# A third buffer for scan states, narrower room for background work on ScalarE, and wider rows in DRAM, in a fused four-layer kernel

## Chip, cores and metric

The kernel runs on one core of one Trainium2 chip. The metric is the device time of one execution in microseconds (us). All data are 32-bit floats. An image is one of the 16 batch entries.

## The reference

Four layers follow each other, each of the form x + layer(group norm of x), on x of 16 x 192 x 32 x 32. Only layers 1 to 3 bear on this change. Cut to what matters:

```python
x = x + _L0_conv_ref(_gn(x), ...)      # gated recurrent block, 3x3 convolution, batch norm
x = x + _L1_conv_ref(_gn(x), ...)      # channel attention: 1x1 and depthwise 3x3 convolutions
x = x + _L2_conv_ref(_gn(x), ...)      # selective scan, below
x = x + _L3_conv_ref(_gn(x), ..., 4)   # softmax over rolled copies of x, 1x1 convolution, gelu

# inside layer 2: xs is xx in K = 4 directions, 384 channels, N = 16 states, L = 1024 steps
x_dbl = einsum('bkdl,kcd->bkcl', xs, x_proj_w)
dts, Bs_, Cs_ = split(x_dbl, [R, R + N], axis=2)
delta = softplus(einsum('bkrl,kdr->bkdl', dts, dt_w) + dt_b)
def step(h, xs_t):
    d_t, u_t, B_t, C_t = xs_t
    dA = exp(d_t[..., None] * A)
    h = h * dA + (d_t * u_t)[..., None] * B_t[:, :, None, :]
    y = einsum('bkdn,bkn->bkd', h, C_t)
    return (h, y)
```

## The kernel before

Layer 0 is run first for all images. The rest is the class `LayersB`. `prepare` (L1132) makes, for one image, layer 1 and the start of layer 2, up to the scan's input `xx` (after a Gelu) and the gate `z`. The scan follows. `complete` (L1358) makes the end of layer 2 and layer 3.

The scan of one image is 192 slots (`UNITS`, L748): 4 directions x 24 groups of 16 channels x 2 blocks of 8 states. A slot is one scan instruction on 128 x 1024. Its partitions are 16 channels x 8 states and its free axis is the 1024 steps. Two slots, an even "first" one and an odd "second" one, make a pair and share a group of channels. Per pair the engines do this, each engine in the order of the program:

- SyncE loads `dl` and `du` (`load_group`, L1793): 16 rows of 4 KB in DRAM, each read 8 times, 512 KB into SBUF each. The two loads for a later pair are issued in the second slot (`fetch`, L1802).
- ScalarE makes `dA` = exp(`dl` x A) for each slot, two slots ahead (`decay`, L1835), and copies `du` into one of the two PSUM buffers `xt` (`inputs_up`, L1831). This copy is issued in the second slot and can begin when the scan of the first slot has read that buffer.
- VectorE multiplies `xt` by the state inputs `bb` twice (L1842), then runs the two scans into `h` (L1851). There are two buffers `h`.
- GpSimd multiplies `h` by the state outputs `cb` into `hc` (L1863, three buffers), one slot behind the scan.
- TensorE sums `hc` over the states into `acc` (L1893), two slots behind. ScalarE copies `acc` out (L1903) every fourth slot.

The scan of image b runs beside the background: `prepare` of image b + 1 and `complete` of image b - 1, two Python generators ("streams") that are cut into pieces by `yield`. A piece names the engine that it uses next. The order of all instructions is written out when the program is built (`scans`, L1618), and the engines follow it: a piece that is emitted in a slot stands behind that slot's own work on its engine. There is no choice at run time.

The planner keeps a clock in us for each engine. `SLOT` (L754) is the planned length of the first and the second slot (4.83 and 2.31), `RATES` in `Metered` (L764) the planned cost of an instruction. `fits` (L1687) lets a piece into a slot if its engine's clock is under the slot's end plus `OVER` (one number for first slots, one for second), if its input is due, with `LEAST` us to spare, before that end, and for TensorE and VectorE if the slot's budget `ALLOW` is not yet spent. An early loop (L1633) lets ScalarE pieces in ahead of the slot's own work by the same test. Pieces marked "late" (those with Tanh or Gelu) go into second slots only.

Two due times are not left to `fits`. In slot 161 of an image (`FETCH`, L749), the loop at L1664 emits all pieces of `prepare` of the next image that are still outstanding, up to its Gelu of `xx`, because `fetch_xx` (L1354) then loads `xx` for the next scan. In slot 144 the loop at L1668 emits all pieces of `complete` up to its second read of `yd`, because the scan overwrites `yd` from there on. After the last slot of the last image the loop at L1680 emits what is left of `complete` of the image before. One background stream has one PSUM bank (`mm`, L836), so a matmul group of a stream waits until ScalarE or VectorE has read the one before.

Steps of the next direction (`front`, L1728: projection, softplus into `dlh`, product into `duh`, stores to `dld` and `dud`) are placed at fixed slots. They use `e`, `dlh` and `duh`, 2 KB per partition each.

Of the kernel before, what the change touches and what calls it, by code (L numbers as in the profile page):

```python
# [11 lines left out]
F32 = mybir.dt.float32  # L12
# [7 lines left out]
C, H, W = 192, 32, 32  # L20
L = H * W
HL = L // 2
P6 = 96
# [4 lines left out]
K, N, R = 4, 16, 12  # L28
# [13 lines left out]
class Ctx:  # L42
# [22 lines left out]
    def ln_exp(self):  # L65
# [4 lines left out]
        if self.ordered:  # L70
            self.spent["ACT"] += TABLE
        i = self.nc.scalar.preload_act_table_set("natural_log_exp_and_others")
# [672 lines left out]
BLOCKS = N // NBL  # L745
# [8 lines left out]
SLOT = (4.83, 2.31)  # L754
OWN = {"POOL": 2.36, "SUMS": 0.6, "START": 0.9, "INPUTS": 1.0, "DECAY": 1.15, "COLLECT": 0.57}
ENGINES = ("PE", "ACT", "POOL", "DVE")
ALLOW = {"PE": 2.45, "DVE": 0.3}
OVER = {"PE": (0.8, 1.2), "ACT": (0.0, 1.5), "POOL": (0.5, 1.5)}
LEAST = {"PE": 1.0, "ACT": 0.6, "POOL": 0.8}
TABLE = 1.28  # L760
MARGIN = 0.6


class Metered:  # L764


    RATES = {"ACT": (0.07, 0.00105), "POOL": (0.1, 0.0022), "DVE": (0.08, 0.00105), "PE": (0.06, 0.0017)}
    LEAST = {"ACT": 0.2, "POOL": 0.2, "DVE": 0.12, "PE": 0.4}

# [3 lines left out]
    def __getattr__(self, op):  # L773
        f = getattr(self.engine, op)

        def issue(out, *args, **kw):
            base, each = self.RATES[self.name]
            self.spent[self.name] += max(self.LEAST[self.name], base + each * math.prod(out.shape[1:]))
            if op == "activation" and args[1] in (AF.Tanh, AF.Gelu):
                self.spent["ACT"] += TABLE * self.cx.has_ln  # L780
                self.cx.has_ln = False
# [43 lines left out]
class LayersB:  # L825
# [44 lines left out]
    def run(self):  # L870
        tc, NB = self.tc, self.NB
        self.bank, self.turn = None, 0
        with ExitStack() as ctx:
# [4 lines left out]
            self.xp = ctx.enter_context(tc.tile_pool(name="b_x", bufs=1, space=PSUM))  # L878
            self.spent, self.have = dict.fromkeys(ENGINES, 0.0), dict.fromkeys(ALLOW, 0.0)
            self.clock = dict.fromkeys(ENGINES, 0.0)  # L880
# [26 lines left out]
    def setup(self):  # L907

        tc, nc, cx, wp, I, NB = self.tc, self.nc, self.cx, self.wp, self.I, self.NB
        dp = self.dp  # L910
        self.dqd = dp.tile([6, 128, 9, 128], F32, name="dqd")
        self.dvd = dp.tile([2, 2, P6, 9, P6], F32, name="dvd")
        self.vd = dp.tile([P6, 2, L], F32, name="vd")
        self.x0d = dp.tile([P6, 2, L], F32, name="x0d")
        self.x2d = dp.tile([P6, 2, L], F32, name="x2d")
        self.xdr = dp.tile([K, 2 * N, L], F32, name="xdr")
        self.dld = dp.tile([K, 3, 128, L], F32, name="dld")
        self.dud = dp.tile([K, 3, 128, L], F32, name="dud")
        self.xxd = dp.tile([3, 128, L], F32, name="xxd")
        self.yd = dp.tile([3, 128, L], F32, name="yd")  # L920
        self.zd = dp.tile([NB, 3, 128, L], F32, name="zd")
        self.x1d = dp.tile([NB, P6, 2, L], F32, name="x1d")


        bn_g, bn_b = self.vec("bn_g", P6), self.vec("bn_b", P6)
        self.bsc = wp.tile([P6, 2], F32, name="bsc")
        self.bsh = wp.tile([P6, 2], F32, name="bsh")
        with tc.tile_pool(name="b_pre0", bufs=1) as pre:
            st = pre.tile([P6, 2, NB, 12], F32, name="st")
            for a in range(2):  # L930
                nc.scalar.dma_start(
                    st[:, a], self.sdram[:, a * P6 : (a + 1) * P6, :].rearrange("b p s -> p b s")
                )
            mv = pre.tile([P6, 2, 2], F32, name="mv")
            for a in range(2):
                nc.vector.bn_aggr(mv[:, a, :], st[:, a].rearrange("p b s -> p (b s)"))
            sd = pre.tile([P6, 2], F32, name="sd")
            nc.scalar.activation(sd, mv[:, :, 1], AF.Sqrt, bias=cx.eps5[0:P6])
            nc.vector.reciprocal(sd, sd)
            nc.vector.tensor_mul(self.bsc, sd, bn_g)  # L940
            nc.vector.tensor_mul(sd, mv[:, :, 0], self.bsc)
            nc.vector.tensor_sub(self.bsh, bn_b, sd)


        self.offb = wp.tile([P6, P6], F32, name="offb")
        nc.sync.dma_start(self.offb, I["c_off48"])
        self.temp = wp.tile([P6, 2], F32, name="temp")
        for a in range(2):
            for j in range(2):
                nc.sync.dma_start(  # L950
                    self.temp[48 * j : 48 * j + 48, a : a + 1],
                    I["temperature"][2 * a + j : 2 * a + j + 1].unsqueeze(0).to_broadcast([48, 1]),
                )

        self.dw2b = self.vec("dw_b", 128)
        self.pads = [wp.tile([128, H + 2, W + 2], F32, name="pad%d" % i) for i in range(2)]
        for t in self.pads:
            nc.gpsimd.memset(t, 0.0)

        self.xx = wp.tile([128, 3, L], F32, name="xx")  # L960
    def setup_scans(self):

        nc, cx, wp, I = self.nc, self.cx, self.wp, self.I
# [50 lines left out]

        ring = lambda name, n, shape: [wp.tile(shape, F32, name=name + str(i)) for i in range(n)]
        self.y = wp.tile([128, 3, L], F32, name="y")
        self.dA, self.h, self.hc = ring("dA", 3, [128, L]), ring("h", 2, [128, L]), ring("hc", 3, [128, L])
        self.dl, self.du = ring("dl", 2, [128, L]), ring("du", 2, [128, L])
        self.bb, self.cb = ring("bb", BLOCKS, [128, L]), ring("cb", 3, [128, L])
        self.e, self.dlh, self.duh = (wp.tile([128, HL], F32, name=n) for n in ("e", "dlh", "duh"))  # L1020
        self.xd = wp.tile([64 + XR, L], F32, name="xd")
        self.dtw = wp.tile([64 + R, INNER], F32, name="dtw")
        self.xt = [self.xp.tile([128, L], F32, name="xt%d" % i) for i in range(2)]
# [108 lines left out]
    def prepare(self, b):  # L1132

        nc, cx, sm, I = self.be, self.cx, self.sm, self.I
# [42 lines left out]
        for m in range(3):  # L1177
# [5 lines left out]
            elif m == 1:  # L1183
                w1 = self.weight(self.w1d, [P6, 2, C])
            else:
                wpf = self.weight(I["w_projfT"].rearrange("(a p) o -> p a o", p=P6), [P6, 2, C])
# [13 lines left out]

        id6 = cx.ident[0:P6, 0:P6]
        at = sm.tile([P6, 2, P6], F32, tag="at", name="at", bufs=1)
        kk = sm.tile([P6, 2, C], F32, tag="m1", name="kk", bufs=1)[:, :, 0:P6]
        rq = sm.tile([P6, 2], F32, tag="rq", name="rq")
        vs = [self.p4([P6, 2, HL], "vh") for _ in range(2)]
        for hf in range(2):
# [19 lines left out]
        for a in range(2):  # L1226
# [5 lines left out]
                nc, pk[:, ch(a)], [(qT[:, t, k0 : k0 + P6], qT[:, t, k0 : k0 + P6]) for t in range(NCH)]  # L1232
            )
        yield "DVE", 0
        nc.vector.tensor_mul(
            kk, pk.rearrange("p (a c) -> p a c", a=2), id6.unsqueeze(1).to_broadcast([P6, 2, P6])
        )
# [34 lines left out]
        yield "ACT", 0  # L1272
        for a in range(2):
            nc.scalar.mul(at[:, a, :], at[:, a, :], den[:, a : a + 1])
        m1 = sm.tile([P6, 2, C], F32, tag="m1", name="m1", bufs=1)
        m2 = sm.tile([P6, 2, C], F32, tag="m2", name="m2", bufs=1)
        for m_, w_ in ((m1, w1), (m2, wpf)):
            yield "PE", 0
            p = self.mm()[0:P6, 0 : 2 * C]
            for a in range(2):  # L1280
                nc.tensor.matmul(p[:, a * C : (a + 1) * C], lhsT=at[:, a, :], rhs=w_[:, a, :], start=True, stop=True)
            yield "ACT", 0
            nc.scalar.copy(m_, p.rearrange("p (a c) -> p a c", a=2))
        ds = [self.taps(P6, self.dvd[1, 0], I["dw_kv"][ch(0)], b == 0)]
        for hf in range(2):
            for a in range(2):
# [331 lines left out]
    def scans(self, b, more, carry):  # L1618
# [9 lines left out]
        for t in range(UNITS):  # L1628
# [30 lines left out]
            for e in ENGINES:  # L1659
                clock[e] += self.spent[e] - was[e]  # L1660
            for e in ALLOW:
                have[e] = min(have[e], 0.0) + ALLOW[e] - self.spent[e] + was[e]
            if more and t == FETCH:
# [23 lines left out]
    def fits(self, s, end):  # L1687

        if not s.open(self.slots) or s.engine == "SP":
            return s.engine == "SP" and s.open(self.slots)  # L1690
        at = self.clock[s.engine]
        if s.engine != "DVE":
            end += OVER[s.engine][self.slots % BLOCKS]
        wait = s.inputs()
        if wait > at and (s.engine == "DVE" or wait + LEAST[s.engine] > end):
            return False
        return at < end + 0.1 and self.have.get(s.engine, 1.0) > 0.0

# [145 lines left out]
    def scan(self, u):  # L1844
        nc = self.nc
        n, blk = divmod(u, BLOCKS)
        k = n // GROUPS
        views = [self.h[u % 2], self.dA[u % 3], self.xt[(n + 1 + blk) % 2]]
        if k >= 2:
            views = [v[:, ::-1] for v in views]  # L1850
        nc.vector.tensor_tensor_scan(*views, 0.0, op0=ALU.mult, op1=ALU.add)  # L1851

    def outputs(self, u, carried=False):

        n, blk = divmod(u, BLOCKS)

        k = n // GROUPS - K * (carried and u == UNITS - 1)
        views = [self.hc[u % 3], self.h[u % 2], self.c_of(k, blk)]
        if n // GROUPS % 2:
            views = [views[0].rearrange("p (h w) -> p w h", w=W)] + [  # L1860
                v.rearrange("p (w h) -> p w h", h=H) for v in views[1:]
            ]
        self.nc.gpsimd.tensor_mul(*views)  # L1863
# [139 lines left out]
```

## Time and profile before

| What | us |
|---|---|
| Median of 3 runs (15584.52 to 15626.19) | 15609.16 |
| Profiled execution, its own time | 15591.93 |
| Profiled execution, its span | 15590.1 |
| First scan of layers 1 to 3 starts at | 3545.2 |
| Last scan of layers 1 to 3 ends at | 15451.2 |
| From the last scan's end to the end of the span | 138.9 |
| Granted TensorE clock, mean over the span | 0.838 |

The 3072 scans take 11906 us, so a pair of slots takes 7.75 us on average; the median pair takes 7.42 us and the fastest tenth 6.83 us. Before them lie layer 0, the un-interleaved `prepare` of image 0 and the first steps of its scan; after them `complete` of the last image. In the profile, most background instructions have line L782, that of the helper that records their cost, and have to be told apart by their tiles. A matmul of 32-bit floats has two records, so 18 records on `pad` are one half of a 3x3 depthwise convolution (9 matmuls).

### The profile page before, as it was taken

To read this page: it belongs to the slowest core of one execution; us is meant where nothing else is said; L and a number is where in the kernel's file an instruction comes from. 1 tells how busy PE (TensorE), PEld (TensorE's weight loads), DVE (VectorE), ACT (ScalarE), POOL (GpSimd) and SP (SyncE) were. 2 spreads that over 40 slices of the span, in tenths; PEclk is the share of its full clock that TensorE was granted. 3 is DMA by queue.
4 is the path that set the end of the run, shared out by engine and by line. 5 is a ranking of instruction groups with operands and counts; after the bars stand their busy time and mean duration, and the time that the engine had idled before them with its cause. 6 is when DMAs were issued, how large, how long until landed. Compare 5 with 4: busy or idle time off the path is not lost. (4 is left out here: it accounts for less than half of the span.)

```text
span 15590.1 us, 196674 instructions
## 1 busy us (share of the span) xinstructions
PE 12621.5 (81%) x72384; PEld 5045.6 (32%) x72384; DVE 12310.8 (79%) x10295; ACT 9263.9 (59%) x12084; POOL 9861.8 (63%) x5787
## 2 busy tenths in 40 slices
PE   9999999987787777877787777877787777878755
PEld 5555555542222222222222222222222222222212
DVE  4444444448988999999989898898989898988997
ACT  3333333326666666666666666666666666666665
POOL 1000000006787878787878787878878787878785
PEclk9999999997787888878788888887888887878766
DMA  1000000017777787878787878787777787777775
GB/s 29 12 15 14 15 14 15 15 40 189 201 195 200 188 207 188 210 182 214 182 211 183 213 184 211 183 210 189 202 194 198 194 202 195 199 195 193 201 182 129
DMA packets 852126, 2412.70 MB, mean 155 GB/s; under 512 B 114352, under 2 KB 234240, under 8 KB 843520
## 3 DMA queue, kind: packets, MB, share of 16 engines
q1 hardware_dynamic: 838496, 2397.64, 60.2%
q8 instruction: 580, 9.50, 0.3%
q10 hardware_dynamic: 12704, 2.72, 0.1%
q14 instruction: 346, 2.83, 0.1%
HBM read 2018.92 MB, written 364.30 MB: 153 GB/s over the span
## 5 line engine op out<-in xcount | busy, mean ns | idle before, releaser
L1863 POOL TENSOR_TENSOR hc<-h,cb 128x1024 f32<-128x1024 f32 x3072 | 7247.3, 2371 | 2046.2 <-DVE h L1851 1557.8
L1851 DVE TENSOR_TENSOR_SCAN h<-dA,xt 128x1024 f32<-128x1024 f32 x3072 | 6912.8, 2273 | 297.0 <-POOL hc L1863 289.1
L1842 DVE TENSOR_TENSOR xt<-xt,bb 128x1024 f32<-128x1024 f32 x3072 | 3633.4, 1227 | 852.7 <-ACT xt L1831 718.9
L1835 ACT ACTIVATE dA<-dl,A 128x1024 f32<-128x1024 f32 x3072 | 3506.7, 1146 | 801.2 <-DMA dl<-dld 672.8
L1893 PE MATMUL acc<-hc,sel 128*32 128x256 f32 x24576 | 2406.8, 473 | 1707.6 <-POOL hc L1863 1705.0
L782 PE MATMUL mm<-pad,dg 128*128 128x512 f32 (+1 forms) x5580 | 2899.3, 655 | 13.3 <-ACT pad L782 9.9
L1831 ACT COPY xt<-du 128x1024 f32<-128x1024 f32 x1536 | 1557.6, 1014 | 1361.7 <-DVE h L1851 1183.5
L1893 PEld LDWEIGHTS acc<-hc,sel 128*32 128x32 f32 x24576 | 562.2, 120 | 4055.4 <-POOL hc L1863 2897.2
L782 PEld LDWEIGHTS mm<-pad,dg 128*128 128x128 f32 (+1 forms) x5580 | 995.5, 192 | 1479.2 <-issue 1363.3
L596 POOL TENSOR_TENSOR vw<-va,gtok 128x396 f32<-128x396 f32 x112 | 95.2, 850 | 1712.0 <-ACT va L588 1712.0
L782 PE MATMUL mm<-x,wgt 96*128 96x512 f32 (+1 forms) x1664 | 1064.5, 775 | 140.1 <-ACT o L782 50.0
L1884 PE MATMUL acc<-y,ident 128*128 128x512 f32 x576 | 445.7, 866 | 445.5 <-ACT y L1903 444.5
L782 POOL TENSOR_TENSOR t<-x 96x768 f32<-96x768 f32 (+4 forms) x510 | 647.5, 1290 | 204.6 <-PE mm L782 204.2
L691 POOL TENSOR_TENSOR x_in<-x_in,sz 128x384 f32<-128x384 f32 x128 | 116.8, 913 | 750.5 <-DVE x_in L687 676.7
L782 PE MATMUL mm<-d,xT 128*96 128x256 f32 x2048 | 569.1, 416 | 5.6 <-ACT o L782 5.3
L782 PEld LDWEIGHTS mm<-x,wgt 96*128 96x128 f32 (+1 forms) x1664 | 342.1, 226 | 669.9 <-issue 364.5
L782 POOL TENSOR_TENSOR duh<-dlh,xx 128x512 f32<-128x512 f32 x384 | 537.5, 1400 | 30.1
L782 POOL TENSOR_TENSOR dlh<-dlh,e 128x512 f32<-128x512 f32 x384 | 488.4, 1272 | 103.1 <-ACT e L782 101.2
L782 PE MATMUL mm<-xd,dtw 12*128 12x512 f32 x768 | 534.5, 782 | 10.0 <-ACT z L782 10.0
L622 DVE TENSOR_TENSOR D<-D,s 128x256 f32<-128x256 f32 x768 | 270.8, 415 | 322.6 <-ACT D L619 322.6
L389 PE MATMUL pc<-ypad,w_c 128*64 128x512 f32 (+1 forms) x1152 | 442.9, 633 | 80.4 <-PEq L735 41.3
L619 ACT ACTIVATE D<-s 128x256 f32<-128x256 f32 x768 | 232.7, 390 | 426.3 <-PE s L613 426.3
(331 smaller groups left out, 15374.9 us busy)
## 6 DMA issues: line engine op xcount, KB each, us to landing
dl<-dld SPq DMA_DIRECT2D x1536, 512.0 KB
du<-dud SPq DMA_DIRECT2D x1536, 512.0 KB
dld<-dlh SPq DMA_DIRECT2D x384, 256.0 KB
dud<-duh SPq DMA_DIRECT2D x384, 256.0 KB
bb<-xdr SPq DMA_DIRECT2D x128, 512.0 KB
cb<-xdr SPq DMA_DIRECT2D x128, 512.0 KB
dg<-dqd SPq DMA_DIRECT2D x270, 192.0 KB
zd<-z SPq DMA_DIRECT2D x48, 512.0 KB
```

The lines of the kernel that those rows point to most:

```text
L389: nc.tensor.matmul(p[r, :], lhsT=w_, rhs=v, start=(n == 0), stop=(n == 14))
L619: nc.scalar.activation(d, S[j][:, two], AF.Exp)
L622: nc.vector.tensor_mul(d, d, S[j][:, 2 * CH :])
L691: nc.gpsimd.tensor_mul(hT[:, :, cs], hT[:, :, cs], sz[:, :, cs])
L782: return f(out, *args, **kw)
L1831: self.nc.scalar.copy(self.xt[n], self.du[n])
L1835: self.nc.scalar.activation(self.dA[u % 3], self.dl[n % 2], AF.Exp, scale=self.A[:, blk, n : n + 1])
L1842: self.nc.vector.tensor_mul(self.xt[(n + 1 + blk) % 2], self.xt[n % 2], self.bb[blk])
L1851: nc.vector.tensor_tensor_scan(*views, 0.0, op0=ALU.mult, op1=ALU.add)
L1863: self.nc.gpsimd.tensor_mul(*views)
L1884: nc.tensor.matmul(acc, lhsT=self.cx.ident, rhs=self.y[:, g, half(pair)], start=True, stop=False)
L1893: nc.tensor.matmul(self.acc[rows4(q), q4(s)], lhsT=self.sel[:, m, :], rhs=self.hc[u % 3][:, q4(q)], start=False, stop=(s + m + blk == 3),)
```

## The change

There are five edits.

1. `h` gets a third buffer, and `scan` and `outputs` take `h[u % 3]`.
2. Room in SBUF is made for it: `e` becomes the same buffer as `duh`; the small tile `kk` moves to the slot "pa", and `m1` and `m2` move to the ring "w" of two weight buffers, which holds `w1` and `wpf` before them and `wx` and `wz` after them.
3. The planner's numbers for ScalarE in first slots change: a piece must find ScalarE's clock 0.6 us before the slot's end where the end itself was enough, and an input that comes later than the clock must be due 1.6 us before that, where it was 0.6.
4. TensorE's budget per slot goes from 2.45 to 3.0 us.
5. Rows of `xdr`, `dld` and `dud` in DRAM lie 36 KB apart (`PITCH` = 9 rows of 4 KB), where they were 4 KB apart. The bytes that are moved stay the same.

```diff
-ALLOW = {"PE": 2.45, "DVE": 0.3}
-OVER = {"PE": (0.8, 1.2), "ACT": (0.0, 1.5), "POOL": (0.5, 1.5)}
-LEAST = {"PE": 1.0, "ACT": 0.6, "POOL": 0.8}
+ALLOW = {"PE": 3.0, "DVE": 0.3}
+OVER = {"PE": (0.8, 1.2), "ACT": (-0.6, 1.5), "POOL": (0.5, 1.5)}
+
+LEAST = {"PE": (1.0, 1.0), "ACT": (1.6, 0.6), "POOL": (0.8, 0.8)}
 TABLE = 1.28
+PITCH = 9
...
-        self.xdr = dp.tile([K, 2 * N, L], F32, name="xdr")
-        self.dld = dp.tile([K, 3, 128, L], F32, name="dld")
-        self.dud = dp.tile([K, 3, 128, L], F32, name="dud")
+
+        self.xdr = dp.tile([K, 2 * N, PITCH, L], F32, name="xdr")[:, :, 0, :]
+        self.dld = dp.tile([K, 3, 128, PITCH, L], F32, name="dld")[:, :, :, 0, :]
+        self.dud = dp.tile([K, 3, 128, PITCH, L], F32, name="dud")[:, :, :, 0, :]
...
-        self.dA, self.h, self.hc = ring("dA", 3, [128, L]), ring("h", 2, [128, L]), ring("hc", 3, [128, L])
+        self.dA, self.h, self.hc = ring("dA", 3, [128, L]), ring("h", 3, [128, L]), ring("hc", 3, [128, L])
...
-        self.e, self.dlh, self.duh = (wp.tile([128, HL], F32, name=n) for n in ("e", "dlh", "duh"))
+        self.dlh, self.duh = (wp.tile([128, HL], F32, name=n) for n in ("dlh", "duh"))
+        self.e = self.duh
...
-        kk = sm.tile([P6, 2, C], F32, tag="m1", name="kk", bufs=1)[:, :, 0:P6]
...
+        kk = self.slot("pa", [P6, 2, P6], "kk")
...
-        m1 = sm.tile([P6, 2, C], F32, tag="m1", name="m1", bufs=1)
-        m2 = sm.tile([P6, 2, C], F32, tag="m2", name="m2", bufs=1)
-        for m_, w_ in ((m1, w1), (m2, wpf)):
+
+        ms = []
+        for w_ in (w1, wpf):
...
+            m_ = self.slot("w", [P6, 2, C], "m", 2)
+            ms.append(m_)
             nc.scalar.copy(m_, p.rearrange("p (a c) -> p a c", a=2))
+        m1, m2 = ms
...
-        if wait > at and (s.engine == "DVE" or wait + LEAST[s.engine] > end):
+        if wait > at and (s.engine == "DVE" or wait + LEAST[s.engine][self.slots % BLOCKS] > end):
             return False
...
-        views = [self.h[u % 2], self.dA[u % 3], self.xt[(n + 1 + blk) % 2]]
+        views = [self.h[u % 3], self.dA[u % 3], self.xt[(n + 1 + blk) % 2]]
...
-        views = [self.hc[u % 3], self.h[u % 2], self.c_of(k, blk)]
+        views = [self.hc[u % 3], self.h[u % 3], self.c_of(k, blk)]
```

## The prediction

> **What bounds the kernel now.** I read the busy times of the stretches first. The scan loop runs from 3545.2 to 15451.2 us; the row above it is the un-interleaved `prepare` of image 0. Columns: length, then busy us of TensorE, its weight loads, VectorE, ScalarE, GpSimd (instructions in brackets), granted TensorE clock, DMA share, GB/s.
>
> ```profile
> 3354.00:3518.00 164.00, 147.34 (x393) 67.24 (x394) 85.68 (x157) 41.77 (x77) 0.21 (x1) 0.92 0.20 59
> 3545.20:15451.20 11906.00, 9189.66 (x42510) 3203.20 (x42510) 10736.22 (x7133) 7882.74 (x9506) 9524.81 (x5243) 0.80 0.77 196
> ```
>
> VectorE is busy for 10736 of 11906 us. It is the bound, and what can be won is its idle time. The waits of VectorE in that window say who ends it (total, times, longest):
>
> ```profile
> DVE xt L1842 <- ACT xt L1831: 689.2, 355, 8.1
> DVE h L1851 <- POOL hc L1863: 289.1, 229, 3.3
> DVE yh L782 <- PE mm L782: 36.8, 16, 3.3
> DVE xt L1842 <- DMA bb<-xdr: 17.7, 32, 3.2
> ```
>
> With the small rows this is 1039 us. The 289 us are scans that wait for a free `h`. The 689 us are the copy of `du` being late on ScalarE. The timeline shows how that comes about (start, length, instruction, idle time before it and who ended it):
>
> ```profile
> 4640.88 5.43 PE L782 MATMUL mm<-pad,dg 96*96 96x512 f32 x6
> ...
> 4646.35 0.58 ACT L782 COPY vf<-mm 96x512 f32<-96x512 f32 x1 [8.73 <-PE mm L782]
> ...
> 4646.83 1.02 ACT L1831 COPY xt<-du 128x1024 f32<-128x1024 f32 x1
> ...
> 4647.88 2.36 DVE L1842 TENSOR_TENSOR xt<-xt,bb 128x1024 f32<-128x1024 f32 x2 [7.04 <-ACT xt L1831]
> ```
>
> A background copy stands ahead of the scan's copy on ScalarE and waits 8.73 us for a convolution on TensorE; VectorE then idles 7.04 us. I went through the 355 waits this way: some 430 us have ScalarE waiting for TensorE in a background piece, 55 us have it waiting for `dl`.
>
> [...] a record on `pad` takes 592 ns in the median and up to 1223. [...] Edit 5 goes from 4 to 36 KB, [...] and no run here shows it. [...]
>
> **Part by part. Third `h`.** The scan may now be one slot further ahead of GpSimd, at least 2.3 us (one scan, 2273 ns). Of 229 waits three quarters are under 1.95 us, and the longest is 3.3. About 60 of the 289 us stay. It goes on to wait for GpSimd only when GpSimd is two slots late.
>
> **ScalarE in first slots.** The copy gets at least 1.0 to 1.6 us more slack before a background piece. Taking 1.6 us off each of the 355 waits leaves 278 of 689 us. In the order of the changed kernel's instructions, some 460 background ScalarE pieces are let into first slots by `fits`, where 706 were; 278 x 460 / 706 = 180. With 60 for the other rows (yh, bb, small ones), 60 + 180 + 60 = 300 of 1039 us stay. Bounds: 150 (all waits for ScalarE go) to 600 (TensorE, up to 8 us late, is too late for 1.6 us to matter).
>
> **What that order also shows.** A stricter door slows both streams; TensorE's larger budget (3.0) does not help a stream that waits for ScalarE. Counted between the sums of two neighbouring slots, the kernel before never has more than 9 background matmuls. The changed kernel keeps to 11 in images 0 to 4, then falls behind, and the due times empty the streams at one place:
>
> - slot 161 (`prepare` is due): 20, 40, 68, 94, 122, 124, 112, 124, 124, 124 matmuls in images 5 to 14
> - slot 144 (`complete` is due): 37, 53, 83, 83, 83, 13 in images 10 to 15
> - after the last slot: 156
>
> In the kernel before, no piece is forced by a due time. A forced block is one dependent chain: one bank for each stream, so TensorE waits for ScalarE's copy, ScalarE for TensorE. TensorE's next sums, ScalarE's next `dA` and copy, and VectorE's next scan (behind the block's own VectorE pieces) are queued behind it. VectorE can run two more slots under a block at 161 and one under a block at 144, because their `dA` and `xt` were emitted before it; then it stands still.
>
> Price of a matmul of 512 columns, from `prepare` of image 0 (36 records are 18 matmuls, 15.62 / 18 = 0.87 us):
>
> ```profile
> 3446.97 15.62 PE L782 MATMUL mm<-pad,dg 96*96 96x512 f32 x36
> ...
> 3482.80 7.89 PE L782 MATMUL mm<-pad,dg 128*128 128x512 f32 x18
> ```
>
> TensorE: by columns the blocks at 161 make 17 + 35 + 57 + 80 + 103 + 104 + 96 + 3 x 104 = 804 us, those at 144 make 25 + 32 + 3 x 49 + 11 = 215. That is 1019 us at full clock and 1108 at the 0.92 of the stretch alone. ScalarE: 197 and 81 forced pieces, at 0.58 us for a copy of 512, 1.05 to 1.23 for 1024 wide, 1.28 for a table load: 183 + 78. VectorE: 48. GpSimd: 133, mostly beside TensorE because those pieces are pipelined; a third counts, 45. Handovers: some 680 changes of engine at 0.12 us, the mean of 0.04 (TensorE to ScalarE) and 0.2 (back) as the last `complete` shows them: 82. Sum 1108 + 261 + 48 + 45 + 82 = 1544. Off it come ten times 7 us and seven times 2.3 us of scans that run under a block (86), and VectorE's 48, which the loop's busy time already holds: 1410 us.
>
> A check on one block: 3438.5 to 3518 us is about the block of 124 matmuls, made alone, 79.5 us, with half of five convolutions on VectorE beside TensorE. Put back on TensorE they add 5 x (7.89 + 0.58) = 42, together 122 us with three banks in turn; my sum has about 150 for one bank. So the low bound is 0.82 of the sum: 1544 x 0.82 - 134 = 1130. The high bound takes TensorE at the loop's clock of 0.80: 1410 + 166 = 1576.
>
> **The end.** 156 matmuls by columns 66 us, ScalarE 27, a part of GpSimd's 50 and handovers: 110 us (90 to 130), after the last scan and so all on the path.
>
> **`fetch_xx` after a block.** `xxd` is written only at the block's end, so SyncE waits for that store before it can load `xx`, and the next `dl` and `du` stand behind it on SyncE's queue. 1.5 MB out and in at the loop's 196 GB/s is 8 + 8 us, of which about 10 us of scans hide most: 6 us a block, 60 us (0 to 120).
>
> **The rest.** `e` in `duh`: the next `e` is written three slots after `duh`'s store was issued, some 11 us: nothing; were the store later, ScalarE would wait. `kk`, `m1`, `m2` in other slots: `wx` and `wz` load after `m1` and `m2` were read, once an image, and SyncE waits a few us with `dl` behind it: within the bounds above. Row pitch: the waits of VectorE that a faster `dl` or `bb` would end are 55 + 18 us, so at best -70; at worst the loads slow until they bind, which I bound by +100. I take nothing.
>
> **Sum.** 15592 (the profiled execution) - 1039 + 300 + 1410 + 110 + 60 = 16433 us. The median of the runs lies 17 us above the profiled one: 16450. Low: 15592 - 1039 + 150 + 1130 + 90 + 17 = 15940. High: 15592 - 1039 + 600 + 1576 + 130 + 120 + 17 = 16996.
>
> **Rivals.**
> - *Faster: the blocks are mostly hidden.* In images 5 and later the planner's clocks stay ahead after a block, so dozens of slots carry no background and TensorE is free there. If the engines could begin a block well before VectorE reaches its slot, 60 in 100 of it would be under scans: 15592 - 1039 + 300 + 0.4 x 1580 + 17 = 15502. It decides once blocks, end and fetch cost under 739 - 17 us together. Against it: the block stands behind sums of slot 159, which need its scan, so it cannot begin early. 0.06.
> - *Half clock in the blocks.* [...] TensorE's 1019 us double (2340 instead of 1410) and its 66 at the end too: 15592 - 1039 + 300 + 2340 + 176 + 60 + 17 = 17446. Against it: the stretch alone held 0.92. 0.08.
> - *The door does not help.* ScalarE's waits stay because TensorE is late by much more than 1.6 us: 750 instead of 300 stay, 16900. For it: waits up to 8.1 us. Against it: later images have less background outside the blocks. 0.14.
>
> **How the numbers follow.** My forecast, with sizes between its bounds, has 0.72. The range 15950 to 16980 holds it but for its tails, and the third rival; outside lie the first two rivals and some tails, 2 in 10. Within 0.3% of 15609 (about what a measurement of this kernel can tell from no change) needs gain and blocks to cancel: 0.03, out of the low tail. Faster 0.06, slower 0.91.
>
> **What would show it.** Right: in images 0 to 4 the scan takes some 30 us less than the 748 us that an image took before (by the starts of every 192nd scan); in images 9 to 14 it takes 100 to 200 us more; VectorE has a few idle stretches of 60 to 150 us near slots 144 and 161; the time from the last scan to the end grows from 139 to about 250; the row of `h` waiting for `hc` falls under 100 us. Wrong: if those stretches are under 40 us each, or if the first five images don't get shorter.

## The result, and the profile after

| Kernel | Median us | Runs | Ratio to before, 95% interval |
|---|---|---|---|
| before | 15599.7 (15584.52 to 15626.19) | 4 | |
| changed | 17019.26 (17004.21 to 17028.31) | 4 | 1.0897 [1.0884, 1.091] |

The change makes the kernel 1420 us slower. The forecast was 841 us slower than the 15609 it started from; the measured time lies 39 us above its range.

First the busy times of two stretches of the changed kernel, the scan loop and what follows it. The columns are those of the prediction.

```profile
3545.70:16760.20 13214.50, 9293.80 (x42216) 3256.72 (x42220) 10699.57 (x7127) 7892.17 (x9468) 9468.89 (x5178) 0.75 0.68 177
16760.20:17011.70 251.50, 168.79 (x708) 85.17 (x700) 47.43 (x83) 82.38 (x121) 77.79 (x108) 0.72 0.09 27
```

The loop is 1308.5 us longer and the end 112.6 us longer; that is the whole loss. VectorE's work is 37 us less than before (10736), so what grew is its idle time, from 1170 to 2515 us. Its waits in the loop (total, times, longest):

```profile
DVE xt L1849 <- ACT xt L1838: 1456.5, 400, 78.6
DVE x L784 <- PE mm L784: 507.8, 49, 62.2
DVE yh L784 <- PE mm L784: 340.1, 12, 74.1
DVE xt L1849 <- DMA bb<-xdr: 32.7, 30, 9.7
DVE h L1858 <- POOL hc L1870: 29.6, 31, 3.4
```

Two things stand out. The row of `h` waiting for `hc` fell from 289 to 29.6 us. And the first three rows have longest waits of 62 to 79 us, where the longest before was 8.1. Sorted by length, 31 idle stretches of VectorE of over 9 us hold 1468 us, where there was none; all shorter ones hold 1047 us. Of the 31, 29 with 1449 us lie ahead of the scans of slots 145, 162 and 164, right behind a due time; the other two are under 10 us each. By row, the shorter waits for the copy are 393 with 762 us. That is more than before (359 with 691), not the 180 us of the forecast.

The page's slices (40 equal parts of the span, busy tenths of VectorE, then the granted TensorE clock) show where it goes: the first images look alike, and from the middle on VectorE falls back again and again.

```profile
DVE  4444444379889988898888787968585949577684
...
PEclk9999999987877878877777787877677776768666
```

The same by images, from the start of every 192nd scan to the next:

```text
image    0      1      2      3      4      5      6      7      8      9      10     11     12     13     14     15
after  718.3  746.6  750.5  765.4  751.9  767.2  779.0  823.8  846.4  841.3  931.2  917.5  941.5  945.4  952.5  735.8
```

Before, the images from the second to the eighth took 742 to 756 us. Images 9 to 14 are 93 to 205 us over the 748 us of the forecast's comparison, close to the 100 to 200 expected; image 0 is shorter, images 1 to 4 are not. One of the long stretches, from the timeline of image 13 at slot 161 (VectorE's instructions around it, others left out):

```profile
14811.91 4.46 DVE L1858 TENSOR_TENSOR_SCAN h<-dA,xt 128x1024 f32<-128x1024 f32 x2
...
14875.42 0.68 DVE L784 TENSOR_TENSOR x<-x,mm 96x512 f32<-96x512 f32 x1 [59.05 <-PE mm L784]
...
14890.56 4.45 DVE L1858 TENSOR_TENSOR_SCAN h<-dA,xt 128x1024 f32<-128x1024 f32 x2
...
14973.50 2.37 DVE L1849 TENSOR_TENSOR xt<-xt,bb 128x1024 f32<-128x1024 f32 x2 [78.49 <-ACT xt L1838]
```

VectorE runs four scans and a few pieces of the block between 14812 and 14895 and otherwise waits, first for a product of TensorE behind four half convolutions, which it has to add to `x`, then for a copy of `du` that stands behind the whole block on ScalarE. TensorE in the same stretch:

```profile
14847.52 7.97 PE L784 MATMUL mm<-pad,dg 96*96 96x512 f32 x18 [0.67 <-ACT vf L784]
14856.15 7.97 PE L784 MATMUL mm<-pad,dg 96*96 96x512 f32 x18 [0.67 <-ACT vf L784]
...
14956.94 7.99 PE L784 MATMUL mm<-pad,dg 128*128 128x512 f32 x18 [0.68 <-ACT xg L784]
14965.73 1.50 PE L1900 MATMUL acc<-hc,sel 128*32 128x256 f32 x24
```

One convolution after another, each 0.67 us after the one before, because ScalarE's copy out of the one bank, 0.58 us, lies between them. The sums of the scan (L1900) come only when the block is through. It is the serial chain that the prediction priced. The busy times of this block and of the one at slot 144 of the same image:

```profile
14819.00:14975.00 156.00, 126.63 (x274) 46.16 (x274) 14.23 (x21) 24.62 (x36) 5.45 (x3) 0.85 0.17 48
14662.00:14750.00 88.00, 52.91 (x154) 28.17 (x154) 2.55 (x4) 20.23 (x25) 27.21 (x40) 0.79 0.24 69
```

TensorE is busy 81% of the longer one at a granted clock of 0.85. That is a mean of two levels. Three parts of the same block:

```profile
14819.00:14840.50 21.50, 18.43 (x20) 5.09 (x21) 0.00 (x0) 2.66 (x5) 0.69 (x1) 0.50 0.53 125
14841.00:14885.00 44.00, 37.57 (x84) 12.76 (x82) 3.43 (x6) 2.33 (x4) 0.00 (x0) 1.00 0.03 8
14885.50:14905.50 20.00, 13.96 (x19) 5.43 (x20) 8.80 (x14) 4.38 (x8) 2.37 (x1) 0.50 0.21 60
```

In the first 22 us of the block, four products and the start of a convolution with gaps of 0.56 to 0.68 us, the clock was 0.50. Through the chain of convolutions and products after them, with gaps of 0.67 to 0.78 us, it was 1.00. It was 0.50 again for some 20 us from 14885 on, around a group norm that left TensorE idle for 3.60 and 2.23 us; the half convolution that began there took 10.77 us in place of 7.99.

### The profile page after: what moved, and what is told of

The parts are those of the page before. It is cut to its first block, busy times and chain, and to the rows that moved or that the text cites. A ratio compares the mean times of both kernels' runs of the same rounds, so it can differ in the third digit from the quotient of the medians.

```text
span 17011.7 us, 196311 instructions
## 1 busy us (share of the span) xinstructions
PE 12797.0 (75%) x72384; PEld 5137.2 (30%) x72384; DVE 12277.3 (72%) x10295; ACT 9301.3 (55%) x12089; POOL 9858.1 (58%) x5787
## 4 chain that ended last, share of the span: by engine, by line
PE 25%; DVE 17%; issue 14%; POOL 12%; ACT 7%; DMA 7%; SPq 0%; DVEq 0%; ACTq 0%; POOLq 0%
PE mm L784 20%; DVE h L1858 10%; POOL hc L1870 8%; DVE xt L1849 5%; DMA dl<-dld 3%; PE acc L1900 2%; POOL t L784 2%; ACT xt L1838 2%; ACT dA L1842 2%; DMA du<-dud 1%; POOL dlh L784 1%; PE acc L1891 1%; DMA yh<-yd 1%; POOL duh L784 1%; PE pc L389 0%
## 5 line engine op out<-in xcount | busy, mean ns | idle before, releaser
L1858 DVE TENSOR_TENSOR_SCAN h<-dA,xt 128x1024 f32<-128x1024 f32 x3072 | 6878.7, 2270 | 30.9 <-POOL hc L1870 29.6
L1900 PE MATMUL acc<-hc,sel 128*32 128x256 f32 x24576 | 2532.6, 499 | 2573.2 <-POOL hc L1870 2570.6
L784 PE MATMUL mm<-pad,dg 128*128 128x512 f32 (+1 forms) x5580 | 2793.1, 643 | 94.5 <-ACT pad L784 38.7
L1900 PEld LDWEIGHTS acc<-hc,sel 128*32 128x32 f32 x24576 | 594.3, 124 | 4818.8 <-POOL hc L1870 3853.2
L784 PE MATMUL mm<-xd,dtw 12*128 12x512 f32 x768 | 607.7, 881 | 4.9 <-ACT z L784 4.9
L784 POOL TENSOR_TENSOR dlh<-dlh,duh 128x512 f32<-128x512 f32 x384 | 488.9, 1273 | 106.0 <-ACT duh L784 106.0
L784 ACT COPY pad<-mm 128x512 f32<-128x512 f32 (+1 forms) x320 | 186.5, 583 | 525.0 <-PE mm L784 522.0
```

The costliest lines, as they stand in the source:

```text
L784: return f(out, *args, **kw)
L1900: nc.tensor.matmul(self.acc[rows4(q), q4(s)], lhsT=self.sel[:, m, :], rhs=self.hc[u % 3][:, q4(q)], start=False, stop=(s + m + blk == 3),)
```

## The experiments

Where an edit is made to the changed kernel, its lines may be shifted by one or two. "Copy waits" are the waits of VectorE's product for the copy of `du`, "`h` waits" those of the scan for `hc`; both count single waits of up to 9 us in the loop, all longer ones are "long" (in e3, e4 and e12 they are about 11 us each in the mean, all for the copy). The rows of e1, e2, e3, e4, e11 and e13 below take in one wait for the copy of some 34 us that lies ahead of the first scan; the table leaves it out. Forced pieces are counted in the written-out order: those that a due time or the end of the program emits. "e2 setting" means the changed kernel with the planner's old numbers.

| Run | Median us | Ratio, 95% | `h` waits us | copy waits us | long us (n) |
|---|---|---|---|---|---|
| before | 15600 | | 289 | 691 | 0 |
| changed | 17019 | 1.0897 [1.0884, 1.091] | 30 | 762 | 1468 (31) |
| e1 | 15586 | 0.9983 [0.9976, 0.9989] | 37 | 965 | 10 (1) |
| e2 | 15568 | 0.9977 [0.9964, 0.9991] | 40 | 884 | 0 |
| e3 | 15840 | 1.0137 [1.012, 1.0154] | 0 | 1055 | 198 (18) |
| e4 | 15473 | 0.9908 [0.9891, 0.9924] | 0 | 770 | 167 (15) |
| e5 | 15456 | 0.9896 [0.9876, 0.9916] | 43 | 816 | 0 |
| e6 | 15590 | 0.9991 [0.9981, 1.0001] | 42 | 888 | 0 |
| e7 | 15449 | 0.9897 [0.9874, 0.992] | 38 | 818 | 0 |
| e8 | 18179 | 1.1642 [1.1613, 1.1672] | 17 | 563 | 2646 (54) |
| e9 | 15491 | 0.9916 [0.9898, 0.9935] | 17 | 864 | 0 |
| e10 | 15473 | 0.9906 [0.9886, 0.9926] | 224 | 663 | 0 |
| e11 | 15285 | 0.979 [0.9766, 0.9813] | 1 | 700 | 0 |
| e12 | 15467 | 0.9897 [0.9875, 0.9919] | 1 | 793 | 136 (13) |
| e13 | 15295 | 0.9798 [0.9781, 0.9814] | 41 | 632 | 0 |
| e14 | 15341 | 0.9818 [0.9801, 0.9834] | 225 | 546 | 0 |

### Are the blocks the whole loss?

**e1.** After each of the two due-time loops the planner's clock of VectorE is set to the latest clock, so that the plan knows that VectorE stood still during a block. With that it lets the streams run on at once, and in the written-out order no piece is forced; all five edits stay.

```diff
                 while self.parked < b + 2:
                     self.advance(self.after)
+                clock["DVE"] = max(clock.values())
...
                 while self.read < b:
                     self.advance(self.before)
+                clock["DVE"] = max(clock.values())
```

> The changed kernel with one planner line added at each due time: VectorE's planned clock is set to the furthest planned clock there. The built order then has no piece forced by a due time in any image; all else is as in the changed kernel. Theory (the blocks are the loss): their 1468 us of idle VectorE and the 113 us at the end go, and 16 images run like images 1 to 4 of the changed kernel, 754 us each; 17019 - 1468 - 113 + 11 x about 25 for the background that comes back into the slots = about 15710, at most 0.7% above the kernel before. Rival (the third buffer, the shared buffers or the row pitch cost time by themselves and the blocks only mark the place): still above 16200.

Measured: 15586.36 us, 1433 us less than the changed kernel. The waits of VectorE (lines shifted by two):

```profile
DVE xt L1851 <- ACT xt L1840: 1008.2, 489, 34.8
...
DVE h L1860 <- POOL hc L1872: 36.8, 32, 2.1
```

The long waits are gone, and with them the loss. But with every edit in place and no block the kernel is only 0.2% faster than before: the gain of 739 us that the prediction booked isn't there. The waits for the copy have grown, from 691 to 965 us in the table.

**e8.** The changed kernel with the old budget. In the written-out order more is forced, 2160 us of TensorE by the planner's costs, where the changed kernel forces 1178.

```diff
-ALLOW = {"PE": 3.0, "DVE": 0.3}
+ALLOW = {"PE": 2.45, "DVE": 0.3}
```

> The changed kernel with TensorE's budget of 2.45. In the built order the due times force 2502 pieces where the changed kernel has 1264; by the planner's costs 2160 us of TensorE's work instead of 1178. Theory (a forced block is a serial chain that VectorE waits out, so the loss goes with the forced work): the changed kernel lost 17019 - 15586 = 1433 us against e1 for 1178 us, 1.22 us for each us; 15586 + 2160 x 1.22 = about 18220, between 17900 and 18500. Rival (the smaller budget relieves TensorE and pays for its blocks): under 17300.

Measured: 18178.92 us.

```profile
DVE xt L1849 <- ACT xt L1838: 1576.7, 323, 78.7
DVE x L784 <- PE mm L784: 954.3, 77, 62.3
DVE yh L784 <- PE mm L784: 727.4, 13, 80.4
```

The same three rows with the same longest waits as in the changed kernel, in greater number. The changed kernel loses 1433 us (against e1) for 1178 forced, 1.22 per us; e8 loses 2593 against e1 and 2611 against e2 for 2160, 1.20 or 1.21 per us. In these two kernels the loss goes with what is forced.

How a block feeds the next one can be read in the order. After the block at slot 161 of images 7 to 14 VectorE's planned clock stands 87 us behind TensorE's and 94 us behind ScalarE's, since it is moved by VectorE's own pieces alone. For some 50 slots `fits` sees these two as ahead and lets 1 to 18 pieces in, where in images 1 to 3 it lets in 99 to 117, and the next due time finds more left over. e1 cuts just this; at slot 144, where the three clocks already agree, its line changes next to nothing. Neither of the two ScalarE numbers forces anything alone at a budget of 3.0; both together force 1264 pieces.

### Where the gain went

**e2.** The third `h`, the buffer moves and the row pitch, with the planner's old numbers ("e2 setting").

```diff
-ALLOW = {"PE": 3.0, "DVE": 0.3}
-OVER = {"PE": (0.8, 1.2), "ACT": (-0.6, 1.5), "POOL": (0.5, 1.5)}
+ALLOW = {"PE": 2.45, "DVE": 0.3}
+OVER = {"PE": (0.8, 1.2), "ACT": (0.0, 1.5), "POOL": (0.5, 1.5)}
...
-LEAST = {"PE": (1.0, 1.0), "ACT": (1.6, 0.6), "POOL": (0.8, 0.8)}
+LEAST = {"PE": (1.0, 1.0), "ACT": (0.6, 0.6), "POOL": (0.8, 0.8)}
```

> The changed kernel with the planner's three numbers of before (2.45; 0.0; 0.6), so only the third h, the moved small buffers and the row pitch are left. Nothing is forced by a due time. Theory: of the 289 us in which the scan waited for a free h about 260 go, and nothing takes their place: 15600 - 260 = about 15340. Rival 1 (the wait moves to ScalarE's copy, which was late in the same pairs): 15550 to 15600. Rival 2 (e in duh, m1 and m2 in the weight ring cost waits): above 15620.

Measured: 15568.11 us. VectorE's waits:

```profile
DVE xt L1849 <- ACT xt L1838: 916.7, 412, 33.9
DVE yh L784 <- PE mm L784: 47.6, 16, 3.6
DVE h L1858 <- POOL hc L1870: 40.4, 34, 2.0
```

The wait for `hc` falls by 249 us, as forecast, and the wait for the copy rises by 193. It is given back at once: in the 215 pairs of slots that had such a wait of over 0.3 us before, the waits fall from 287 to 3 us and the pairs get 159 us shorter together; the pair after each and the one after that get longer (1773 to 1803 and 1718 to 1807 us in all). Over all pairs within that reach, 34 us are won.

**e6.** The e2 setting with the rows 4 KB apart again: the third `h` alone.

```diff
-PITCH = 9
+PITCH = 1
```

> e2 with the rows of xdr, dld and dud 4 KB apart as before (PITCH = 1). Theory (the pitch is worth the few us by which the 4 KB packets differ, 263 ns before and 258 ns after in images 1 to 4): 15570 to 15640. Rival (the pitch is what made e2 faster and the third h gives nothing or costs): above 15650; or the pitch costs: under 15520.

Measured: 15590.38 us, and the interval of its ratio reaches 1.0001. The third `h` with its buffer moves can't be told from nothing. Between e6 and e2 the pitch makes 22 us by the medians of two sets of runs, but the intervals of their ratios overlap. In images 1 to 4 the packets of 4096 bytes took 261 ns in the mean in e2 and 263 in e6 (263 in the kernel before, 258 in the changed one).

**e3.** The changed kernel with the old ScalarE numbers: the budget of 3.0 on top of e2.

```diff
-OVER = {"PE": (0.8, 1.2), "ACT": (-0.6, 1.5), "POOL": (0.5, 1.5)}
+OVER = {"PE": (0.8, 1.2), "ACT": (0.0, 1.5), "POOL": (0.5, 1.5)}
...
-LEAST = {"PE": (1.0, 1.0), "ACT": (1.6, 0.6), "POOL": (0.8, 0.8)}
+LEAST = {"PE": (1.0, 1.0), "ACT": (0.6, 0.6), "POOL": (0.8, 0.8)}
```

> The changed kernel with the two ScalarE numbers of before (0.0; 0.6): third h, pitch and TensorE's budget of 3.0. Nothing is forced. Theory (the larger budget makes TensorE later, so ScalarE's copies wait more: in images 1 to 4 these waits rose from 180 to 271 us): e2 plus about 23 us an image = about 15700. Rival (it is the ScalarE numbers that raise them): as e2, about 15340.

Measured: 15840.43 us.

```profile
DVE xt L1849 <- ACT xt L1838: 1286.6, 483, 33.6
DVE xt L1849 <- DMA bb<-xdr: 65.7, 36, 7.6
```

Under the old ScalarE numbers the budget costs 272 us against e2. Inside the waits for the copy, the part in which ScalarE stands idle for TensorE in a background piece grows from some 180 to some 315 us. The prediction let the budget pass as harmless.

**e4.** The changed kernel with the 1.6 back at 0.6; the other new number, the slot's end less 0.6, stays.

```diff
-LEAST = {"PE": (1.0, 1.0), "ACT": (1.6, 0.6), "POOL": (0.8, 0.8)}
+LEAST = {"PE": (1.0, 1.0), "ACT": (0.6, 0.6), "POOL": (0.8, 0.8)}
```

> The changed kernel with 0.6 instead of 1.6 as the least time for an input, so of the stricter ScalarE rule only the -0.6 is left, with the budget of 3.0. Nothing is forced. Theory (planned slack doesn't reach a TensorE that is several us late): within 0.5% of e3. Rival (the rule works, and only the blocks hid it): 200 to 350 us under e3.

Measured: 15473.26 us.

```profile
DVE xt L1849 <- ACT xt L1838: 968.1, 415, 34.4
DVE xt L1849 <- DMA bb<-xdr: 22.0, 32, 1.9
```

367 us less than e3. After e3 I held that ScalarE's numbers don't matter, since TensorE's lateness sets the waits; that fell. The 0.6 us at the end of first slots work; adding the 1.6 us to it is what brings the blocks.

**e10 and e7.** The rule of 0.6 us with a budget of 2.6, once in the kernel before (two `h`, rows 4 KB apart), once in the changed kernel.

```diff
-ALLOW = {"PE": 2.45, "DVE": 0.3}
-OVER = {"PE": (0.8, 1.2), "ACT": (0.0, 1.5), "POOL": (0.5, 1.5)}
+ALLOW = {"PE": 2.6, "DVE": 0.3}
+OVER = {"PE": (0.8, 1.2), "ACT": (-0.6, 1.5), "POOL": (0.5, 1.5)}
```

> The kernel before with two planner numbers of e7 alone: ScalarE's -0.6 in first slots and TensorE's budget of 2.6. Two h, rows 4 KB apart, no shared buffers; the plan is piece for piece that of e7. Theory (the end rule is what gains, the third h hardly): 15449 + 20 for h + 20 for the pitch = 15470 to 15520. Rival (with the copies earlier the third h is worth what it was meant to be, since its gain is no longer taken back): 15600 to 15700.

```diff
-ALLOW = {"PE": 3.0, "DVE": 0.3}
+ALLOW = {"PE": 2.6, "DVE": 0.3}
...
-LEAST = {"PE": (1.0, 1.0), "ACT": (1.6, 0.6), "POOL": (0.8, 0.8)}
+LEAST = {"PE": (1.0, 1.0), "ACT": (0.6, 0.6), "POOL": (0.8, 0.8)}
```

> e4 with TensorE's budget at 2.6 instead of 3.0, still with nothing forced by a due time. Theory (the larger budget alone cost 272 us in e3 against e2, the end rule alone gave 367 in e4 against e3): the rule without most of the budget's cost, 15250 to 15400. Rival (the rule only repairs what the budget spoilt): 15450 to 15580, between e4 and e2.

Measured: 15472.54 us and 15448.65 us. The rule gives nearly all of it without the third `h`; the third `h` and the pitch add 24 us, and the two intervals overlap. e7 was expected at 15250 to 15400 and lies only 25 us under e4: beside the rule a budget of 3.0 costs little more than one of 2.6, so the 272 us of e3 hold for the old ScalarE numbers alone.

### What makes the copy late

**e5.** The e2 setting with six of the nine matmuls of each half convolution on TensorE left out, their planned cost kept, so that the order of the rest stays.

```diff
+                if t % 4:
+                    self.spent["PE"] += 0.06 + 0.0017 * HL
+                    continue
```

> e2 (third h, pitch, planner of before) with 6 of the 9 matmuls of each half convolution on TensorE left out (taps 0, 4 and 8 stay), charged to the planner as if they were there, so that every piece stands in the slot where it stood. The output is not the reference's. Theory (ScalarE's copies are late because TensorE is late in the background): of the 884 us in which VectorE waits for the copy at most a third stays, 15568 - 600 = about 14950. Rival (ScalarE's own queue, or the loads of dl, make the copies late): above 15350.

Measured: 15456.01 us. The busy times of the loop, e2 and then e5:

```profile
3546.00:15400.00 11854.00, 9146.65 (x42468) 3188.30 (x42466) 10688.71 (x7123) 7884.52 (x9508) 9506.14 (x5240) 0.80 0.76 197
```

```profile
3546.00:15400.00 11854.00, 8261.74 (x39072) 2691.05 (x39072) 10723.19 (x7185) 7897.66 (x9536) 9500.13 (x5236) 0.73 0.76 197
```

TensorE is relieved of 885 us, and the copy waits fall only from 884 to 816. Late convolutions are a small part of them; the other background matmuls of TensorE stayed. Of the 112 us that e5 is faster, 36 lie ahead of the loop in the profiled executions, where the convolutions of image 0 are thinned too.

**e9.** The e2 setting with two of GpSimd's background instructions, a sum and a product, made on 128 of 512 columns, their planned cost kept.

```diff
-            nc.gpsimd.tensor_add(self.dlh, self.dlh, self.e)
-            o, x, d = self.duh, self.xx[:, g, half(hf)], self.dlh
+            nc.gpsimd.tensor_add(self.dlh[:, 0:128], self.dlh[:, 0:128], self.e[:, 0:128])
+            o, x, d = (t[:, 0:128] for t in (self.duh, self.xx[:, g, half(hf)], self.dlh))
...
+            self.spent["POOL"] += 2 * 0.0022 * 384
```

> e2 with the two GpSimd products of each front step (into dlh and duh) made on 128 of their 512 columns, charged to the planner in full, so every piece stands where it stood. The output is not the reference's; 384 x 2 x about 1.0 = 770 us of GpSimd's work are left out. Theory (the third h's gain was given back because GpSimd, late in those pairs, reaches VectorE by a second way: hc, sums on TensorE, the background matmuls behind them, ScalarE's pieces, the copy): VectorE's wait for the copy falls from 884 to under 550 us, time about 15200. Rival (ScalarE's own background alone makes the copy late): above 15480.

Measured: 15491.0 us. GpSimd's column falls from 9506 to 8878 us:

```profile
3546.00:15400.00 11854.00, 9142.45 (x42571) 3190.10 (x42570) 10717.25 (x7158) 7896.19 (x9525) 8878.30 (x5244) 0.81 0.76 197
```

By the medians of two sets of runs e9 is 77 us under e2, but the copy waits go only from 884 to 864 us. This part of GpSimd's load isn't what makes the copy late either.

**e13 and e14.** `dl` and `du` are loaded for half of their columns in the loop, and the other half keeps older values; all instructions stay. e13 is the e2 setting, e14 the kernel before with its two `h`.

```diff
+            w = L if full else HL
...
-                t, src[k, g, i * CW : (i + 1) * CW, :].unsqueeze(1).to_broadcast([CW, NBL, L])
+                t[:, 0:w], src[k, g, i * CW : (i + 1) * CW, 0:w].unsqueeze(1).to_broadcast([CW, NBL, w])
```

> e2 (third h, pitch, planner of before) with dl and du loaded for half of their columns only in the loop (256 KB instead of 512 KB each); the other half keeps the rows of two groups earlier. The output is not the reference's; the plan and every computing instruction are those of e2. Theory (the third h gave its gain back because the next pairs are paced by the loads of dl, which ScalarE's dA and all behind it wait for; followed back 14 us, more of the time before the late copies ends in those loads than anywhere else): the waits for the copy fall from 884 to under 600 us, time 15568 - 300 = 15270 or less. Rival (the loads are late beside something else that is as late): above 15480.

> The kernel before with the same halved loads. The output is not the reference's. Theory: with the loads out of the way the third h is worth most of its 289 us, so this run lies 150 to 290 us above e13. Rival (something else takes the gain back): less than 80 us above e13.

Measured: 15294.56 us and 15340.78 us. The loop of e13, with the DMA share down from 0.76 to 0.43, then its waits of VectorE (lines shifted by one), then ScalarE's wait for `dl` in e2 and in e13:

```profile
3546.00:15400.00 11854.00, 9133.14 (x42918) 3196.28 (x42916) 10751.81 (x7211) 7933.74 (x9587) 9547.47 (x5285) 0.81 0.43 130
```

```profile
DVE xt L1850 <- ACT xt L1839: 664.5, 335, 34.2
...
DVE h L1859 <- POOL hc L1871: 40.8, 38, 2.0
```

```profile
ACT dA L1842 <- DMA dl<-dld: 685.3, 248, 8.1
...
ACT dA L1843 <- DMA dl<-dld: 266.8, 142, 3.7
```

So halving the loads takes 274 us off by the medians of e2 and e13, and 272 us between the kernel before and e14, in one set of runs, though hardly any wait of VectorE names them: `dA` waits for `dl`, and the copy of `du` stands behind `dA` on ScalarE. e13 was expected under 15270 us with copy waits under 600 and missed both by some 30. Halved loads take the DMA share of the whole loop down with them, so other transfers may have gained too, and the share of `dl` alone isn't shown. ScalarE's wait for `dl` and the copy waits fall together, from 685 to 267 and from 884 to 632 us. But the third `h`, with the pitch, is worth only 46 us here too (e14 to e13), with 184 us of `h` waits gone and 86 us more of copy waits. The loads are therefore a cost of their own, and not what takes its gain back.

### A better version

**e11 and e12.** e7 with less room for GpSimd's background pieces; e12 goes further with a budget of 2.8.

```diff
-ALLOW = {"PE": 3.0, "DVE": 0.3}
-OVER = {"PE": (0.8, 1.2), "ACT": (-0.6, 1.5), "POOL": (0.5, 1.5)}
+ALLOW = {"PE": 2.6, "DVE": 0.3}
+OVER = {"PE": (0.8, 1.2), "ACT": (-0.6, 1.5), "POOL": (0.0, 1.0)}
...
-LEAST = {"PE": (1.0, 1.0), "ACT": (1.6, 0.6), "POOL": (0.8, 0.8)}
+LEAST = {"PE": (1.0, 1.0), "ACT": (0.6, 0.6), "POOL": (0.8, 0.8)}
```

> e7 with GpSimd's pieces let 0.5 us less over the end of a slot (0.0 and 1.0 instead of 0.5 and 1.5). Nothing is forced by a due time. Theory (GpSimd's lateness is a source of the waits): 15250 to 15400. Rival (it is not, and pieces only move): within 0.4% of e7's 15449.

```diff
-ALLOW = {"PE": 3.0, "DVE": 0.3}
-OVER = {"PE": (0.8, 1.2), "ACT": (-0.6, 1.5), "POOL": (0.5, 1.5)}
+ALLOW = {"PE": 2.8, "DVE": 0.3}
+OVER = {"PE": (0.8, 1.2), "ACT": (-0.6, 1.5), "POOL": (0.0, 0.5)}
...
-LEAST = {"PE": (1.0, 1.0), "ACT": (1.6, 0.6), "POOL": (0.8, 0.8)}
+LEAST = {"PE": (1.0, 1.0), "ACT": (0.6, 0.6), "POOL": (0.8, 0.8)}
```

> As e11, with GpSimd at 0.0 and 0.5 and TensorE's budget at 2.8, the tightest rule for GpSimd that I found without forced pieces. Theory: GpSimd's tighter rule (less waiting) against the larger budget (272 us for 0.55 in e3, so about +100 for 0.2): 15300 to 15500. Rival (the budget decides): above 15520.

Measured: 15285.2 us for e11, which beats both kernels (0.979 [0.9766, 0.9813]), and 15467.17 us for e12. The main row of e11:

```profile
DVE xt L1849 <- ACT xt L1838: 732.4, 376, 33.7
```

`h` waits are at 1 us. Copy waits are at 700, the lowest of all runs with three `h` and whole loads, e8 apart, whose blocks fill the time. e12, with the larger budget, has 13 waits of some 10 us. Why the place of GpSimd's pieces does what less of their work (e9) doesn't isn't shown. In the written-out order of e11 other pieces move too (`fits` lets 700 pieces of ScalarE into first slots, 607 in e7), so the gain can't be put down to GpSimd alone.

## Why the prediction was right in its sign and short in its size

**Forced blocks: right.** 1410 us and 60 for `fetch_xx` were forecast, 1468 us stand in the 31 long stretches (1449 in the 29 behind a due time), and e1 shows that without them the loss is gone. That the total is so close is in part luck, since two sizes inside the sum were off against each other: TensorE ran at a clock of 0.85 and 0.79 in the blocks shown, not 0.92, and a handover from TensorE over ScalarE's copy of 0.58 us and back cost 0.67 us, 0.09 more than the copy and not 0.24. The stretches are shorter than one block each, up to 79 us, because VectorE's own pieces split them. In the block shown, ScalarE's first `dA` after the fetch waited 4.1 us for `dl`, where 6 us a block were taken.

**End: right.** 251.5 us where about 250 were forecast.

**Third `h`: right in its row, wrong as a gain.** 30 us stay where 60 were expected. That the 229 us would be won was an error: in e2 the next two pairs take most of it back, and e6 has no gain that can be told from nothing.

**ScalarE in first slots: the step that failed.** "Taking 1.6 us off each of the 355 waits leaves 278 of 689 us", and with fewer pieces 180. Measured: 762 us of copy waits, 582 more than forecast. A sign of being wrong that the prediction named came true: images 1 to 4 did not get shorter. Four things are wrong with the step.
- The number 1.6 isn't a slack that every piece gets. It only turns pieces away whose input comes later than ScalarE's clock. In the written-out order of images 1 to 4 the planned end of first-slot ScalarE pieces moved, in the median, from 1.55 to 1.88 us ahead of the slot's end, 0.33 us.
- The two parts of the gain were added as if they were independent. The rule of 0.6 us with a budget of 2.6 and two `h` leaves 663 of 691 us (e10), and the third `h` alone raises these waits to 888 (e6).
- The budget of 3.0 was taken as no help and no harm. Under the old ScalarE numbers it costs 272 us (e3). How much of that the changed kernel paid isn't shown, for beside the rule of 0.6 us it costs only 25 us more than 2.6 (e4 and e7). In images 1 to 4, which have no block, the slots with 4 us or more of planned background matmuls go from 20 to 58, the time in which ScalarE stands idle for TensorE inside a copy wait of up to 9 us from 49 to 75 us, and all copy waits from 180 to 271; the `h` waits fall from 72 to 15. So these images took 3014 us and not 30 us less each than their 2991 before.
- All copy waits were taken to shrink alike, most of them put down to late TensorE. The 430 us of the prediction count such waits in full; inside the copy waits of the kernel before, ScalarE stands idle for TensorE in a background piece for 160 us. e5 shows that late convolutions are a small part, e13 that late loads are a larger one.

**The sum.** The idle time apart from the long stretches fell from 1170 to 1047 us, 123 instead of the 739 that were booked: 616 us missing, nearly all of it the 582 of the copy. The blocks with the fetch are 2 us under their forecast, the end 3 over, VectorE's work 37 less: 616 - 2 + 3 - 37 = 580, the difference between the forecast of 16433 for a profiled execution and the 17013.5 of this one.

**Rivals.** That the blocks are hidden is out. That they run at half clock throughout is out too: in the block shown the clock was 0.50 for some 47 of 156 us and 1.00 for the rest, and handovers of 0.67 us stand in stretches of both. The third rival, 750 us of idle time that stay and 16900 us, came nearest. Its number was still too good, since it kept the kernel's old waits for the copy and didn't see that they grow; and its cause, TensorE too late for any such rule, is contradicted by e4, where the 0.6 us rule is worth 367 us.

**What stays open.** What takes back the gain of the third `h` isn't found. The loads don't (e13 and e14); that convolutions or GpSimd's load do is made unlikely by e5 and e9, whose copy waits hardly fall, but neither has a partner with two `h`. ScalarE's own copy of 1.01 us makes up about 40% of a copy wait, and in the program a copy can't begin before the scan of the first slot is done: in the kernel before, 1184 of the 1362 us that ScalarE idles ahead of these copies end with a scan. That this bounds the gain is argued, not shown.

## What to carry to other kernels

When work is placed by a planner, count in the written-out order what a due time forces at one place, and price that as a serial chain with its handovers: here such a price came within some 20 us of 1470, in part by luck, with two terms off against each other. Don't count a wait as won before asking what is late in the same pair of slots and the next two; only the difference to that is a gain. And try each number of a planner alone and in pairs, since two that force nothing alone may tip the plan together.

## What the runs showed that I had not expected

- The third `h` removes nearly 250 us of waits for GpSimd and brings nothing that can be told from no change (e6, 0.9991 [0.9981, 1.0001]).
- Loads that hardly any wait of VectorE names are worth some 270 us when halved (e13 against e2, e14 against the kernel before); ScalarE's wait for `dl` goes from 685 to 267 us.
- 0.6 us at the end of every first slot are worth 367 us with a budget of 3.0 (e3 to e4), and 0.5 us less room for GpSimd's pieces 163 us with a budget of 2.6 (e7 to e11).
- In one chain with gaps of 0.67 to 0.78 us TensorE was granted a clock of 1.00 for 44 us; the 0.85 of the whole block comes from stretches at 0.50, one of them, of 22 us, with gaps of 0.56 to 0.68 us. In the loop of the kernel before, at 77% busy, the mean is 0.80.
